# A list of weights for every step of a planned kernel, the last two token tiles finished singly, and epsilon added on VectorE

## Chip, cores and metric

The kernel runs on one core of a Trainium2 chip. The metric is the device time of one execution in microseconds (us); where several runs are compared, their median. Engines: TensorE (PE, its weight loads PEld), VectorE (DVE), ScalarE (ACT), GpSimd (POOL), SyncE (SP, which issues most transfers).

## What is computed

Two layers of gated cross-attention, each followed by a feed-forward network, on 2 x 1024 tokens of width 256, with a context of 77 tokens, 16 heads of 16. All inputs and outputs are float32. In short:

```python
x = x + tanh(g_xattn[0]) * attn0(layernorm(x), ctx)     # no biases, scale 16 ** -0.5
x = x + tanh(g_ffn[0])   * ffn0(layernorm(x))           # quantised: 256 -> 1024 -> gelu -> 256
x = x + tanh(g_xattn[1]) * attn1(layernorm(x), ctx, distances)   # biases, scores - log(d) * |s|
x = x + tanh(g_ffn[1])   * expert(layernorm(x))

def ffn0(x):     # both weights rounded to {-1, 0, 1} * mean|w|, activations to 8 bits per token
    h = gelu(quant_act(x) @ quant_weight(w1).T)
    return quant_act(h) @ quant_weight(w2).T

def expert(t):   # the router's weights are overwritten with 1 for expert 0
    y = t + relu(t @ w1[0] + b1[0]) @ w2[0] + b2[0]
    return (y - mean(y)) * rsqrt(var(y) + 1e-5) * gamma + beta
```

## The kernel before

**Tiling.** The 2048 tokens are 16 tiles of 128, taken in four groups of four (`GROUPS`, line 47). Each group passes four stages: attention of layer 0 (stage 0, `attention`, L718), the quantised network (stage 1, `bit_ffn`), attention of layer 1 (stage 2), the expert (stage 3, `expert_ffn`). A group's stages depend on each other; groups depend on one another only through shared buffers and engines.

**Attention.** The normalised tokens are transposed on TensorE (L602), multiplied with the query weights (L742), and for each half of the heads and each tile scored against the keys (L766), 8 heads x 77 keys in one row of 616. The softmax of such a row goes over the engines: bias (VectorE, L805, layer 1) or eviction (layer 0), maximum (VectorE, L814), subtraction (POOL or VectorE, L819), exponential (ScalarE, L828), sum (VectorE, L836), reciprocal (L841), product (POOL or VectorE, L845). The probabilities are transposed (L864), evicted (the helper `evict`, on ScalarE L373), multiplied with the values (L877) and the output weights (L898); VectorE adds the gated result to x (L906).

**Quantised network.** Products at L1069 (bf16) and L1099, gelu on ScalarE (L1077), maxima and rounding on VectorE (L995, L1004, L1050, L1085). **Expert.** Products in float32: the first at L1135 (eight blocks of 128 features, four tiles at once), the second at L1154, tile by tile. Two tiles share one PSUM bank `pp`; when both are done VectorE adds them to the normalised input (L1164), takes the statistics of both (`stats`, L535 and L536), and `inverse_std` (L541) gives one over the standard deviation; two VectorE operations per tile (L1174, L1181) and one store of both tiles on SyncE (L1188) end the pair.

**Inverse standard deviation.** It is one step of the plan on POOL with two operations, used by every normalisation: an addition of epsilon to the variance (L547) and a power of -0.5 (L548). There are 24 such steps: 16 for groups of four tiles and 8 for pairs of the expert.

**The order.** No loop of the code issues anything at once. Every operation is added to a `Plan` as a step with a planned cost, an engine (or two to choose from), what it reads and what it writes. `Plan.order(weight)` then simulates the engines: at each point it takes, on each engine, the steps that could start earliest, and among these the one with the highest weight; a step that needs a buffer waits until one is planned to be free. Weights only choose among steps that could start at the same planned moment. Transfers are taken in the order in which they were added. `Plan.issue` emits all steps in order of planned start, so each engine's instruction queue has the plan's order, and runs it in order, each instruction waiting for its semaphores. The plan's costs set the order only; they are no instructions.

Before, `Plan.best` (L297) makes the weight of a step from its longest chain of costs to the end, plus one number for its stage and group:

```python
weight = {
    s: rank[s] + OFFSET[s.stage[0]][s.stage[1]] - (SLACK if s.slack else 0.0)
    for s in self.steps
}
```

It then orders up to nine times, each time with weights from a backward pass (`Plan.back`) over the last order, and keeps the order with the earliest planned end.

Of the kernel before, what the change touches and what calls it, by code (L numbers as in the profile page):

```python
# [34 lines left out]
def bc(ap, axis, n):  # L35
# [14 lines left out]
T_EV, T_MX, T_SUB, T_DEN, T_MUL = 1, 1, 1, 1, 1  # L50

OFFSET = (
    (430, -41, -43, -161),
    (95, 126, -47, 121),
    (389, -35, -49, -189),
    (5, -32, 3, -328),
)
SLACK = 20.0
PASSES = 8
# [75 lines left out]
class Plan:  # L135
# [129 lines left out]
    def back(self, weight):  # L265


        todo = {s: len(s.before) for s in self.steps}
        ready = {e: [(s, 0.0) for s in self.steps if s.engine == e and not todo[s]] for e in LAG}
        free, ends, table = dict.fromkeys(ready, 0.0), {}, None  # L270
        while len(ends) < len(self.steps):
            best = None
            for e, waiting in ready.items():
                if waiting:
                    first = min(max(at, free[e]) for _, at in waiting)
                    pick = max(
                        (s for s, at in waiting if max(at, free[e]) <= first),
                        key=lambda s: weight[s],
                    )
                    if best is None or first < best[0]:  # L280
                        best = first, pick
            begin, s = best
            ends[s] = free[s.engine] = begin + s.cost
            if s.table and s.table != table:
                ends[s] = free[s.engine] = begin + s.cost + TABLE
                table = s.table
            ready[s.engine] = [w for w in ready[s.engine] if w[0] is not s]
            for a in sorted(s.after, key=lambda a: a.n):
                todo[a] -= 1
                if not todo[a]:  # L290
                    at = max(
                        ends[b] + (LAG[a.engine] if a.engine != b.engine else 0.0) for b in a.before
                    )
                    ready[a.engine].append((a, at))
        return ends

    def best(self):  # L297


        rank, best = {}, None  # L300
        for s in reversed(self.steps):
            rank[s] = s.cost + LAG[s.engine] + max((rank[b] for b in s.before), default=0.0)
        weight = {
            s: rank[s] + OFFSET[s.stage[0]][s.stage[1]] - (SLACK if s.slack else 0.0)
            for s in self.steps
        }
        for _ in range(PASSES + 1):
            done, given = self.order(weight)
            end = max(begin + s.cost for begin, s, _ in done)
            if best is None or end < best[0]:  # L310
                best = end, done, given
            weight = self.back({s: begin + s.cost for begin, s, _ in done})
        _, done, given = best
        for _, s, way in done:
            s.way = way
        return [(begin, s) for begin, s, _ in done], given
# [19 lines left out]
def tile_gated_cross_attention_stack(  # L336
# [204 lines left out]
    def inverse_std(mv, n, shifted=True):  # L541

        r = lazy(sm, [P, n], F32, "rstd", 4)
        shift = lazy(sm, [P, n], F32, "shift", 4)

        def fn():
            nc.gpsimd.tensor_scalar(r.ap, mv.ap[:, :, 1], EPS, None, ALU.add)  # L547
            nc.gpsimd.tensor_tensor(r.ap, r.ap, minus_half.ap[:, :n], ALU.pow)  # L548

        pool(1.4, fn, [mv, minus_half], [r])  # L550
        if shifted:
            dve(
                0.44,
# [562 lines left out]
    def expert_ffn(g):  # L1116
# [30 lines left out]
        for i, t2 in enumerate(both):  # L1147
# [19 lines left out]
            for j in range(2):  # L1167
                stats(tgt[2 * i + j], mv2, j)
# [147 lines left out]
```

## Time and profile before

| | before |
|---|---|
| median of 3 runs | 378.0 us (376.08 to 378.7) |
| the profiled execution's own time | 376.4 us |
| its span, first to last instruction | 374.7 us |
| mean granted TensorE clock | 0.976 |
| instructions | 5887 |
| PE busy | 338.2 us |
| DVE, ACT, POOL busy | 276.2, 244.2, 236.4 us |
| ScalarE table loads | 15, each 1283 ns |

The profile is of one execution. Its page gives busy times, the span in 40 slices (one digit each, in tenths, 9.4 us per slice), the costliest groups of instructions with their line, shape, count, total and mean, and the idle time before them with what ended it. Windows give the busy time of each engine in a stretch, waits say who waited for whom, and the timeline lists instructions in order of time. Matmul records come two to a float32 product; a busy TensorE isn't always one at its peak rate.

### The profile page before, as it was taken

What the parts mean: (1) busy time and instruction counts of PE and PEld (TensorE: products, weight loads), DVE (VectorE), ACT (ScalarE), POOL (GpSimd) and SP (SyncE); (2) the same over time, 40 slices, a digit from 0 to 9 for tenths busy, and PEclk for the clock granted to TensorE, in tenths of its full rate; (3) what the DMA queues carried; (4) which work ended last, traced back from release to release, by engine and by line L of the source; (5) the groups of instructions that cost most, each with busy time, mean ns of one, the idle gap of its engine ahead of it and who ended that gap; (6) DMA issues with size and microseconds to landing.
All of it is one profiled execution on the core that took longest, in us unless ns stands there. A gap on an engine that the chain in (4) does not pass through costs nothing.

```text
span 374.7 us, 5887 instructions
## 1 busy us (share of the span) xinstructions
PE 338.2 (90%) x2156; PEld 213.8 (57%) x2156; DVE 276.2 (74%) x580; ACT 244.2 (65%) x389; POOL 236.4 (63%) x252
## 2 busy tenths in 40 slices
PE   4967798699999699799999999899999998999991
PEld 4534365357555358455655666664488547584581
DVE  2699979999999979999797589995009888245033
ACT  3598799997969999998856374867313455324300
POOL 6599999847869834968997264778005858226011
PEclk9989989899999899999999999999999999999997
DMA  8993203000010000000000000001000000000001
GB/s 244 330 213 44 77 41 114 0 2 0 10 10 2 1 2 0 3 0 2 0 2 1 2 0 3 0 2 56 0 2 0 29 30 0 3 29 28 0 16 43
DMA packets 18131, 12.51 MB, mean 33 GB/s; under 512 B 8628, under 2 KB 17589, under 8 KB 18101
## 3 DMA queue, kind: packets, MB, share of 16 engines
q1 hardware_dynamic: 17012, 11.08, 10.7%
q10 hardware_dynamic: 1088, 1.05, 0.9%
q8 instruction: 17, 0.28, 0.3%
q14 instruction: 14, 0.11, 0.1%
HBM read 9.71 MB, written 2.10 MB: 32 GB/s over the span
## 4 chain that ended last, share of the span: by engine, by line
PE 54%; DVE 29%; ACT 7%; POOL 5%; issue 3%; DMA 1%; POOLq 0%; DVEq 0%; ACTq 0%
PE b L1154 15%; PE b L1135 13%; DVE den L836 5%; PE b L877 5%; DVE mx L814 5%; PE b L864 5%; PE b L898 4%; PE sc L766 3%; DVE st L535 3%; PE b L742 3%; DVE top_h L995 2%; POOL probs L845 2%; POOL probs L819 2%; DVE probs L805 2%; DVE hs L1085 2%
## 5 line engine op out<-in xcount | busy, mean ns | idle before, releaser
L819 POOL TENSOR_TENSOR probs<-probs,mx 128x616 f32<-128x616 f32 x64 | 78.6, 1240 | 31.2 <-DVE mx L814 23.9
L845 POOL TENSOR_TENSOR probs<-probs,den 128x616 f32<-128x616 f32 x64 | 77.5, 1230 | 6.5 <-DVE den L841 5.2
L864 PE MATMUL b<-ident,probs 128*128 128x128 f32 (+1 forms) x320 | 48.1, 288 | 12.9 <-ACT hs L1077 4.0
L1154 PE MATMUL b<-staged,hT 128*128 128x256 f32 x256 | 59.1, 381 | 0.4 <-ACT hT L373 0.4
L1135 PE MATMUL b<-xnT,staged 128*128 128x512 f32 x128 | 57.1, 596 | 0.3 <-ACT xnT L373 0.3
L547 POOL TENSOR_SCALAR rstd<-mv 128x4 f32<-128x4 f32 (+1 forms) x24 | 7.9, 328 | 71.9 <-DVE mv L536 65.8
L836 DVE TENSOR_REDUCE den<-probs 128x8 f32<-128x616 f32 x64 | 49.1, 771 | 5.5 <-ACT probs L828 5.5
L864 PEld LDWEIGHTS b<-ident,probs 128*128 128x128 f32 (+1 forms) x320 | 36.1, 143 | 29.8 <-issue 7.7
L1154 PEld LDWEIGHTS b<-staged,hT 128*128 128x128 f32 x256 | 47.5, 190 | 8.8 <-issue 2.1
L814 DVE TENSOR_REDUCE mx<-probs 128x8 f32<-128x616 f32 x64 | 49.3, 781 | 4.0 <-ACT probs L373 3.1
L373 ACT ACTIVATE pT<-b 128x512 f32<-128x512 f32 (+1 forms) x80 | 43.2, 603 | 3.2 <-PE b L864 2.9
L573 ACT ACTIVATE xn<-x,shift,rstd 128x256 f32<-128x256 f32 x48 | 25.5, 601 | 27.6 <-DVE shift L554 27.6
L1135 PEld LDWEIGHTS b<-xnT,staged 128*128 128x128 f32 x128 | 23.8, 190 | 28.0 <-issue 26.1
L373 ACT ACTIVATE hT<-b,eb_sb 128x512 f32<-128x512 f32 x32 | 21.8, 685 | 24.7 <-PE b L1135 24.6
L742 PE MATMUL b<-xnT,wq_sb 128*128 128x512 f32 x64 | 34.3, 643 | 2.9 <-ACT v L373 2.4
L877 PE MATMUL b<-pT,vbd 128*32 128x512 f32 (+1 forms) x256 | 31.5, 598 | 0.3 <-ACT hqT L1034 0.3
L898 PE MATMUL b<-wo_sb,OT 128*128 128x256 f32 x128 | 30.5, 382 | 0.4 <-DVE x L906 0.4
L805 DVE TENSOR_TENSOR probs<-sc,dbias 128x616 f32<-128x616 f32 x32 | 25.0, 784 | 7.4 <-PE sc L766 7.4
L535 DVE BATCH_NORM_STATS2 st<-x 128x6 f32<-128x256 f32 x64 | 24.9, 416 | 7.0 <-DMA x<-in_x_dram 6.0
L828 ACT ACTIVATE probs<-probs 128x616 f32<-128x616 f32 x32 | 22.8, 718 | 10.9 <-POOL probs L819 10.7
L906 DVE SCALAR_TENSOR_TENSOR x<-b,gates,x 128x512 f32<-128x512 f32 x16 | 11.7, 733 | 24.1 <-PE b L898 24.1
L766 PE MATMUL sc<-kbd,qT 32*128 32x154 f32 x512 | 28.5, 328 | 0.9 <-ACT probs L373 0.6
(100 smaller groups left out, 544.4 us busy)
## 6 DMA issues: line engine op xcount, KB each, us to landing
staged<-in_ew_dram SPq DMA_DIRECT2D x2, 1024.0 KB
out_dram<-x SPq DMA_DIRECT2D x8, 256.0 KB
x<-in_x_dram SPq DMA_DIRECT2D x6, 256.0 KB
staged<-in_fw1T_dram SPq DMA_DIRECT2D x1, 1024.0 KB
staged<-in_fw2T_dram SPq DMA_DIRECT2D x1, 1024.0 KB
dbias<-in_dist_dram SPq DMA_DIRECT2D x1, 616.0 KB
x<-in_x_dram SPq DMA_DIRECT2D x4, 128.0 KB
wk_sb<-in_wkT_dram ACTq DMA_DIRECT2D x1, 256.0 KB
```

The lines of the kernel that those rows point to most:

```text
L373: nc.scalar.activation(out(), src(), AF.Relu if relu else AF.Copy if bias is None else AF.Identity, bias=0.0 if bias is None else bias(), ...
L742: lambda h=h, k=k, pq=pq: nc.tensor.matmul(pq.ap, wq_sb.ap[:, k, h * P : (h + 1) * P], xnT.ap[:, k, :], start=(k == 0), stop=(k == KT - 1),),
L766: nc.tensor.matmul(sc.ap[:, q, j * QK : j * QK + QK], qT.ap[rows, h, at : at + P], kbd.ap[rows, h, b].rearrange("p h s -> p (h s)"), start ...
L814: lambda j, n: nc.vector.tensor_reduce(each(mx, j, n), heads(j, n), AX.X, ALU.max),
L819: lambda e, j, n: e.tensor_tensor(heads(j, n), heads(j, n), bc(each(mx, j, n), 2, SK), ALU.subtract),
L836: lambda j, n: nc.vector.tensor_reduce(each(den, j, n), heads(j, n), AX.X, ALU.add),
L845: lambda e, j, n: e.tensor_tensor(heads(j, n), heads(j, n), bc(each(den, j, n), 2, SK), ALU.mult),
L864: lambda j=j, c=c, m=m, tr=tr: nc.tensor.transpose(tr.ap[:m, j, :], prs[j // 2].ap[:, j % 2, c * P : c * P + m], ident.ap),
L877: nc.tensor.matmul(po.ap[32 * q : 32 * q + 32, :], vbd.ap[: CH[c], b, h, s, :], pTs[c].ap[: CH[c], :], start=(i < 4), stop=(i >= 4),)
L898: nc.tensor.matmul(pp.ap[:, j % 2, :], OT.ap[:, k, j * P : (j + 1) * P], wo_sb.ap[:, k, :], start=(k == 0), stop=(k == KT - 1),)
L1135: lambda f=f, k=k, ph=ph: nc.tensor.matmul(ph.ap, ew1_sb.ap[:, k, f * P : (f + 1) * P], xnT.ap[:, k, :], start=(k == 0), stop=(k == KT - 1),),
L1154: lambda j=j, f=f, pp=pp: nc.tensor.matmul(pp.ap[:, j % 2, :], hT[f].ap[:, j * P : (j + 1) * P], ew2_sb.ap[:, f, :], start=(f == 0), stop= ...
```

## The change

**A weight for each step.** `OFFSET`, `SLACK`, `PASSES`, the chain lengths and `Plan.back` are gone. A list of 2088 numbers between 0 and 1869 gives each step its weight by its number in the order in which steps are added, and the plan is ordered once. The list laid over the steps gives these means:

| stage | group 0 | group 1 | group 2 | group 3 |
|---|---|---|---|---|
| 0, attention of layer 0 | 1613 | 1172 | 946 | 1033 |
| 1, quantised network | 1363 | 1052 | 500 | 1041 |
| 2, attention of layer 1 | 1227 | 1057 | 173 | 485 |
| 3, expert | 789 | 681 | 723 | 220 |

**Planned costs** of some steps are new: transposes 0.13 instead of 0.15 and 0.14, the value products 1.90 instead of 1.97, the first quantised product 0.54 instead of 0.44, and a few on VectorE. Five constants that were all 1 (`T_EV` and others) are written as 1.

**Epsilon.** In `inverse_std` the addition becomes a step of its own on VectorE, ahead of the power on POOL.

**The last two tiles.** Of the last pair of the last group, each tile is added, measured, scaled and stored by itself: the addition, `inverse_std` and the store are issued once per tile, on half the size. All other pairs stay as they were. The steps now name single tiles of the shared buffers as what they touch.

```diff
-OFFSET = (
-    (430, -41, -43, -161),
...
+WEIGHTS = tuple(
+    int(w) for w in """
+1628 1470 1670 1643 995 733 467 1247 1143 1461 1551 1018 1411 1503 1814 1347 1543 1583 1841 1823
...
     def best(self):
...
+        weight = {s: WEIGHTS[s.n] for s in self.steps}
+        done, given = self.order(weight)
...
-    def inverse_std(mv, n, shifted=True):
+    def inverse_std(mv, n, shifted=True, part=None):
...
-        def fn():
-            nc.gpsimd.tensor_scalar(r.ap, mv.ap[:, :, 1], EPS, None, ALU.add)
-            nc.gpsimd.tensor_tensor(r.ap, r.ap, minus_half.ap[:, :n], ALU.pow)
-
-        pool(1.4, fn, [mv, minus_half], [r])
+        at = part or slice(0, n)
+
+        dve(
+            0.12, lambda: nc.vector.tensor_scalar(r.ap, mv.ap[:, at, 1], EPS, None, ALU.add),
+            [(mv, j) for j in range(at.start, at.stop)], [r],
+        )
+        pool(
+            1.0,
+            lambda: nc.gpsimd.tensor_tensor(r.ap, r.ap, minus_half.ap[:, :n], ALU.pow),
+            [minus_half, r], [r],
+        )
...
+            last = g == len(GROUPS) - 1 and i == n // 2 - 1
+            for part in ((slice(0, 1), slice(1, 2)) if last else (slice(0, 2),)):
+                count = part.stop - part.start
+                js = range(2 * i + part.start, 2 * i + part.stop)
+                keys_of = lambda t: [(t, j % 2) for j in js]
                 dve(
+                    0.12 + 0.29 * count,
+                    lambda t2=both[i], pp=pp, part=part: nc.vector.tensor_tensor(
+                        t2.ap[:, part], pp.ap[:, part], t2.ap[:, part], ALU.add
                     ),
+                    keys_of(pp) + keys_of(both[i]), keys_of(both[i]),
+                )
+                for j in js:
+                    stats(tgt[j], mv2, j % 2)
+                r2, _ = inverse_std(mv2, count, False, part)
...
+                dma(
+                    0.5,
+                    lambda x2=x_pairs[g][i], part=part, at=(FIRST[g] + js[0]) * P,
+                    count=count: nc.sync.dma_start(
+                        out=out[ds(at, count * P), :].rearrange("(j p) d -> p j d", p=P),
+                        in_=x2.ap[:, part],
                     ),
+                    keys_of(x_pairs[g][i]), [],
+                )
```

## The prediction

> **What bounds the kernel now.** I read the page's busy shares and slices first, then the table of windows, then TensorE's (PE's) waits, and last the timeline of the end.
>
> The page:
>
> ```profile
> PE 338.2 (90%) x2156; PEld 213.8 (57%) x2156; DVE 276.2 (74%) x580; ACT 244.2 (65%) x389; POOL 236.4 (63%) x252
> ...
> PE   4967798699999699799999999899999998999991
> ...
> DVE  2699979999999979999797589995009888245033
> ...
> PEclk9989989899999899999999999999999999999997
> ```
>
> TensorE is nearest to full, but two halves hide in the mean: up to slice 19 (about 180 us) DVE (VectorE) stands at 7 to 9 and PE has holes; after it PE is full and DVE has whole slices of 0 to 3. The windows put numbers on it (length, then busy time of PE, PEld, DVE, ACT, POOL, then clock):
>
> ```profile
> core 0: us, PE busy (x) PEld busy (x) DVE busy (x) ACT busy (x) POOL busy (x), PEclk, DMA share, GB/s
> 0.00:10.00 10.00, 5.25 (x23) 4.52 (x24) 2.67 (x9) 3.06 (x6) 6.50 (x25) 1.00 0.81 242
> 10.00:60.00 50.00, 41.26 (x296) 24.18 (x298) 44.28 (x93) 42.12 (x64) 44.30 (x41) 0.93 0.55 150
> 60.00:90.00 30.00, 26.25 (x227) 15.08 (x223) 28.12 (x54) 28.71 (x46) 20.73 (x25) 0.94 0.01 2
> 90.00:180.00 90.00, 82.29 (x624) 50.00 (x626) 84.32 (x183) 82.09 (x130) 67.77 (x69) 0.98 0.02 3
> 180.00:360.00 180.00, 176.37 (x971) 114.44 (x968) 110.20 (x228) 88.24 (x146) 94.75 (x92) 1.00 0.03 10
> ```
>
> PE idles 4.75 us before the first weights arrive, then 8.7, 3.8, 7.7 and 3.6 us in the four windows that follow, and 7.9 us after its last product (374.7 - 366.8). So 23.8 us lie between its first and last matmul, 20.2 of them before 180 us, where VectorE is 89 to 94% busy and ScalarE 84 to 96%. Up to 180 us the softmax and quantising engines set the pace; after it TensorE does. The longest waits of PE are short and scattered:
>
> ```profile
> PE b L623 <- DMA wk_sb<-in_wkT_dram: 4.8, 1, 4.8
> PE b L864 <- ACT hs L1077: 4.0, 4, 2.3
> PE b L864 <- ACT pT L373: 3.6, 3, 1.4
> PE b L742 <- ACT v L373: 2.4, 1, 2.4
> ```
>
> No single wait can be removed to win much; only other work put into the holes can. That work exists:
>
> ```profile
> L1154 PE MATMUL b<-staged,hT 128*128 128x256 f32 x256 | 59.1, 381 | 0.4 <-ACT hT L373 0.4
> L1135 PE MATMUL b<-xnT,staged 128*128 128x512 f32 x128 | 57.1, 596 | 0.3 <-ACT xnT L373 0.3
> ```
>
> These are the expert products, 116 us, a third of all PE time, with very little work for others. The first one starts at 175.2 us, and the window from 339 to 367 us is group 3's alone: PE 27.8 of 28 us, DVE 7.6.
>
> **Part 1, the weights.** Nothing is removed from any engine; only the order moves. Along the list, group 0 keeps its lead (means 1613, 1363, 1227), its expert products get 1292 (first half) and 641 (second), and what now stands last is layer-1 attention of groups 3 and 2 (485 and 173) and group 2's quantised FFN (500), beside the experts of groups 0, 1, 2 (789, 681, 723). So VectorE-heavy attention of two groups is put late, where VectorE has room (110 of 180 us busy), and PE-only products are offered as fillers as soon as they are ready. That is the direction that the two halves ask for. What it can win at most: the 23.8 us of holes, and the clock that they cost. The granted clock of 0.93, 0.94 and 0.98 on 41.3, 26.3 and 82.3 us busy is 2.9 + 1.6 + 1.6 = 6.1 us. Ceiling: 29.9 us.
>
> How much of it is filled I estimate window by window. 10 to 60 us: only layer 0 is runnable, and DVE, ACT and POOL are all at 84 to 89% there: a quarter of 8.7, 2.2 us. 60 to 90 us: half of 3.8, 1.9 us. 90 to 180 us: attention of several groups can be mixed with the first expert products: two thirds of 7.7, 5.1 us. After 180 us: half of 3.6, 1.8 us. Together 11.0 us. The clock by the same shares: 0.7 + 0.8 + 1.1 = 2.6 us. **Part 1: -13.6 us**, between -29.9 (all filled) and a loss, priced under the rivals. One cost is not in the trace: mixing gelu of one group with exp of another reloads ScalarE's table. Before there are 15 loads at 1283 ns (19 us). Ten more would be 13 us of ScalarE, nothing where it is 49% busy (after 180 us), a hole on PE where it is 91% busy (90 to 180). This I leave in the range.
>
> **Part 2, the last two tiles.** The end of before:
>
> ```profile
> 366.19 0.59 PE L1154 MATMUL b<-staged,hT 128*128 128x256 f32 x2
> 366.89 0.69 DVE L1164 TENSOR_TENSOR xn<-b,xn 128x512 f32<-128x512 f32 x1 [2.94 <-PE b L1154]
> 367.62 0.75 DVE L535 BATCH_NORM_STATS2 st<-xn 128x6 f32<-128x256 f32 x2
> ...
> 368.68 0.37 POOL L547 TENSOR_SCALAR rstd<-mv 128x2 f32<-128x2 f32 x1 [5.64 <-DVE mv L536]
> 369.13 0.81 POOL L548 TENSOR_TENSOR rstd<-rstd,minus_half 128x2 f32<-128x2 f32 x1
> 369.98 0.88 DVE L1181 SCALAR_TENSOR_TENSOR x<-xn,rstd,x 128x256 f32<-128x256 f32 x2 [0.61 <-POOL rstd L548]
> 370.94 0.37 SPq L1188 DMA_DIRECT2D out_dram<-x  x1
> ```
>
> From the last matmul (366.78) to the store's issue (370.94) are 4.16 us. For one tile: hop 0.11; the addition on half the columns 0.42 (0.69 less half of what 128x512 costs over 128x256, by 0.73 at L906 against 0.47 at L1107); one statistic 0.38 and its aggregate 0.15; epsilon on VectorE 0.15; hop 0.09; the power 0.75; hop 0.04; one final product 0.44. Sum 2.53, so -1.6 us. The first of the two tiles has its own chain of 2.5 us under the second tile's 16 matmul records at 0.216 (5.18 us for 24), 3.5 us, and is done in time; it adds an addition, a power and a store, all hidden. SyncE gains one issue of 0.37 us, ahead of the last store but 3 us early. The store itself: from issue to the span's end are 3.76 us for 256 KB, now 128 KB. In proportion to bytes that would be -1.9 us. The Trainium skill (DMA: Bandwidth & Descriptors, Anatomy of one DMA) speaks against this: a fixed 2.0 us, mostly the receipt of the write, and only bytes over 436 GB/s on top, so halving gives -0.3 us (its fit is for transfers issued from GpSimd; these go out on SyncE). No row separates the two; I take -0.3. **Part 2: -1.9 us** (-3.5 by proportion; about 0 if another group's store ends last).
>
> **Part 3, epsilon on VectorE.** Off POOL go 24 operations (7.9 us, mean 328 ns), onto VectorE come 25. Nearest row: the tensor_scalar at L1004, 150 ns on 128x1, 410 ns on 128x4 with two operations; the reciprocal on 128x4 takes 178. I take 0.18: 4.5 us of VectorE in all (3.8 to 10). The chain for the norm loses 0.29 + 0.08 on POOL and gains 0.18, but on VectorE the step queues behind whatever is there, often a reduction of 0.78 us (L814) with ScalarE's normalisation (L573) and so the transposes waiting behind. Some 12 of the 25 lie before 180 us, 2.2 us of an engine at 93%; half of it I count: **+1 us** (-1.5 to +4). A rule would make it worse: the Trainium skill (SBUF — State Buffer, Who interferes with whom) says that tensor_scalar on VectorE can take the port pair shared with GpSimd, and that the later one then blocks for the whole instruction. With POOL busy two thirds of the time in pieces of 1.22 us, each of 25 additions would wait 0.4 us on average, +10 us on VectorE, some +4 on the end. The rows speak otherwise: L1004 is the same operation beside the same POOL, and its 16 instances of 128x1 lie within 123 and 156 ns. I keep the row.
>
> The new planner costs and the folded constants issue no other instruction; their effect is in the order, part 1.
>
> **Sum.** -13.6 - 1.9 + 1.0 = -14.5 us on 376.4 us (span 374.7 and 1.7 around it) gives 361.9. The runs' median of 378.0 lies 1.6 above the profiled execution; made against it, **363 us**.
>
> **The rivals.**
> A, the forecast, 355 to 370 us: chance 0.63. For it: two halves with opposite limits, and 116 us of fillers. Against: the list only ranks steps that could start at the same time, and the chip's queues run in order whatever comes late.
> B, nearly all holes and clock filled: 378.0 - 29.9 - 1.9 + 1 = 347, centre 350: 0.12. Against it: the start, where nothing but layer 0 is runnable.
> C, the holes only move (more table loads, epsilon behind reductions, VectorE still full before 180 us): parts 2 and 3 are left, 377 us: 0.12.
> D, slower: the end becomes VectorE's and POOL's. Eight half-pairs of softmax on layer 1 cost POOL 8 x (1.24 + 1.23) = 20 us and VectorE 8 x 2.5 (0.78 at L805, 0.78 at L814, 0.77 at L836, 0.20 at L841) = 20 us per group; if the expert products of groups 0, 1 and 3 have been used up when group 2's layer-1 attention (weight 173) runs, PE has only that group's own transposes and waits for about half, 10 us, with the same again for group 3, and gains nothing earlier: 378 - 1.9 + 1 + 13 to 20, about 392. It decides once PE's idle time after 250 us (about 2 now) exceeds the 13.6 us gained earlier. For it: weights 173 and 485 stand after the experts. Against: those experts have 116 us to lie beside 40. Chance 0.13.
>
> **Range and chances.** Leaving out the lower half of B (0.07) and D (0.13): 351 to 378. A measurement of this kernel tells about 1% from no change. Faster by over 1%: A, B and a little of C, 0.76; within 1%: 0.12; slower: 0.12.
>
> **What would show it.** Part 1 right: PE idle before 180 us down from 25 (start included) towards 15, PE clock there at 0.97 or more, expert products (L1135's) before 150 us, VectorE busier after 180 us. Part 2: last matmul to store's issue near 2.5 us, issue to end about 3.5. Part 3: VectorE's new additions at 0.15 to 0.2 us. Wrong if the table loads pass 25, if PE waits on attention after 250 us (D), or if before 180 us VectorE is still full and PE as empty as now (C).

## The result and the profile after

The changed kernel takes 382.2 us (median of 4 runs, 381.0 to 384.6) against 378.0: ratio 1.013, interval 1.010 to 1.016. It is 1.3% slower; 363 us and a range that ended at 378 had been forecast. The profiled execution of after is the slowest of its four, 384.6 us with a span of 382.5; that of before, 376.4 us with a span of 374.7, is near the fastest of its own. So the two profiles lie 7.8 us apart, the medians 4.2. The page of after, shares of the span first:

```profile
PE 341.9 (89%) x2147; PEld 215.1 (56%) x2156; DVE 291.8 (76%) x608; ACT 244.5 (64%) x389; POOL 228.5 (60%) x227
...
PE   4975998799798898899999998989999899999992
...
DVE  2698999979999999999856999988238984174033
...
PEclk9996899899899999999999999999999989999998
```

The line to look at is not PE's. ACT stays at 244 us and POOL gives up 7.9 us with the epsilon additions, as reckoned. DVE rises from 276.2 to 291.8 us, by 15.6, and only some 4.5 had been reckoned for the new steps. PE's digits before slice 19 are no fuller than they were. The windows of after, cut as before's were, with one more at the end (length, busy time of PE, PEld, DVE, ACT, POOL, then clock):

```profile
10.00:60.00 50.00, 41.10 (x292) 25.86 (x290) 44.05 (x85) 40.34 (x62) 42.19 (x35) 0.90 0.48 139
60.00:90.00 30.00, 26.88 (x205) 14.35 (x208) 26.71 (x57) 26.88 (x44) 18.92 (x22) 0.94 0.12 26
90.00:180.00 90.00, 79.65 (x611) 49.89 (x614) 86.51 (x185) 81.98 (x129) 63.28 (x61) 0.98 0.01 1
180.00:360.00 180.00, 173.97 (x961) 108.06 (x962) 124.92 (x255) 91.08 (x152) 95.74 (x85) 0.99 0.03 10
```

Between 90 and 180 us PE is busy for 79.7 us where it was busy for 82.3, and DVE for 86.5 of 90 where it was 84.3. Up to 180 us PE idles 27.2 us (25.0 before; 15 was forecast), after it 13.4 (11.5). That is 4.1 us more idle time, of which at most 2 us may be nine products whose records are missing in the trace of after (2147 against 2156, each 0.21 us behind the next). The mean granted clock is 0.976 in the profile of before and 0.969 in that of after, but this belongs to the two executions shown and not to the change: over all executions before was granted 0.961 to 0.976 and after 0.968 to 0.972. The first expert product starts at 176.6 us, where it started at 175.2: no filler reached the holes before 150 us. The table loads are still 15.

TensorE's waits of after, in us in total, times and the longest:

```profile
PE b L914 <- ACT xnT L418: 6.4, 1, 6.4
PE b L673 <- DMA wk_sb<-in_wkT_dram: 4.8, 1, 4.8
PE b L914 <- POOL probs L895: 2.5, 4, 0.9
...
PE sc L816 <- DVE den L891: 2.3, 1, 2.3
```

Two are new. The 6.4 us stand at 26 us, where ScalarE has a logarithm (1.32 us) and two table loads (1.28 us each) ahead of the evictions that PE needs. The 2.3 us stand at 304 us, and lead to VectorE.

**Where VectorE's 15.6 us are.** The same work by line and shape, first in before, then in after (count, busy us, mean ns):

```profile
L1181 DVE SCALAR_TENSOR_TENSOR x<-xn,rstd,x 128x256 f32<-128x256 f32 x16 | 12.1, 795 | 4.6 <-POOL rstd L548 4.6
L1174 DVE SCALAR_TENSOR_TENSOR xn<-xn,mv,gamma_sb 128x256 f32<-128x256 f32 x16 | 8.5, 570 | 0.0
L1050 DVE TENSOR_SCALAR xn<-xn,up_x 128x256 f32<-128x256 f32 x16 | 6.5, 463 | 0.1
L1004 DVE TENSOR_SCALAR top_h<-top_h 128x1 f32<-128x1 f32 x16 | 2.4, 150 | 0.4
L1004 DVE TENSOR_SCALAR top_x<-top_x 128x4 f32<-128x4 f32 x4 | 1.6, 410 | 0.1
```

```profile
L1240 DVE SCALAR_TENSOR_TENSOR x<-xn,rstd,x 128x256 f32<-128x256 f32 x16 | 10.9, 712 | 1.9 <-POOL rstd L598 1.9
L1232 DVE SCALAR_TENSOR_TENSOR xn<-xn,mv,gamma_sb 128x256 f32<-128x256 f32 x16 | 10.1, 648 | 0.3
L1100 DVE TENSOR_SCALAR xn<-xn,up_x 128x256 f32<-128x256 f32 x16 | 9.7, 663 | 0.1
L593 DVE TENSOR_SCALAR rstd<-mv 128x4 f32<-128x4 f32 x16 | 3.7, 230 | 0.4
L895 DVE TENSOR_TENSOR probs<-probs,den 128x616 f32<-128x616 f32 x2 | 3.5, 1806 | 0.0
L593 DVE TENSOR_SCALAR rstd<-mv 128x2 f32<-128x2 f32 x7 | 3.1, 440 | 0.1
L1054 DVE TENSOR_SCALAR top_x<-top_x 128x4 f32<-128x4 f32 x4 | 2.7, 675 | 0.1
```

Of the 15.6 us, some 7 are the new epsilon additions (L593), 3.5 two products of the softmax that the new plan gives to VectorE (L895; none in before), 3.2 the quantising step (L1050, now L1100). One operation on one shape has no fixed duration here: L1100 takes 299 to 1372 ns. Its instances sort by what GpSimd does as they start. Two instances of L604 (128x4) in the timeline of after, each with the GpSimd operation in progress (start, length):

```profile
236.51 1.22 POOL L895 TENSOR_TENSOR probs<-probs,den 128x616 f32<-128x616 f32 x1
236.57 1.17 DVE L604 SCALAR_TENSOR_TENSOR shift<-mv,rstd 128x4 f32<-128x4 f32 x1
```

```profile
136.03 0.31 POOL L1059 TENSOR_SCALAR down_h<-top_h,s_w 128x1 f32<-128x1 f32 x1
...
136.58 0.15 DVE L604 SCALAR_TENSOR_TENSOR shift<-mv,rstd 128x4 f32<-128x4 f32 x1
```

The operation on four elements per partition lasts as long as the rest of GpSimd's softmax, and ends with it. Some instances of after, from the trace's single records (the seven that began during a GpSimd operation all do this):

```
L604, ns            rest of GpSimd's operation    L604 lasted
at 236.57 (L895)    1156                          1173
at 293.05 (L869)     958                           973
at 158.48 (L895)     825                           843
at 184.92 (L1175)    710                           730
at  97.04 (L895)     581                           599
no such operation      0                           109 to 165
```

So VectorE operations of some kinds wait for GpSimd when both read SBUF. That is what the Trainium skill states (SBUF — State Buffer, Who interferes with whom): an instruction of VectorE with two inputs in SBUF contends with one of GpSimd that reads SBUF, and one in a two-port mode is blocked for the whole instruction; a reduction is not. The trace agrees for GpSimd's large operations (its small ones are in the last section): the two-input L604 and L1240, and the tensor_scalar L1100 and L593, last longer by up to 1.1 us; the reductions L864 and L886 stay between 0.74 and 0.80 us beside the same operations. Counted over L604 and the kinds of operation in the rows of after above, 18 of 64 instances in before and 34 of 91 in after last over a quarter longer than when free, beside an operation of GpSimd on 128x616 or 128x512.

The place at 302 us shows how this reaches TensorE. VectorE and GpSimd in after:

```profile
301.46 1.22 POOL L895 TENSOR_TENSOR probs<-probs,den 128x616 f32<-128x616 f32 x1 [0.92 <-DVE den L891]
...
301.90 2.47 DVE L1240 SCALAR_TENSOR_TENSOR x<-xn,rstd,x 128x256 f32<-128x256 f32 x2
302.64 1.45 POOL L1175 TENSOR_TENSOR xn<-xn,eb_sb 128x512 f32<-128x512 f32 x1
304.29 0.78 DVE L864 TENSOR_REDUCE mx<-probs 128x8 f32<-128x616 f32 x1
```

Two final products take 2.47 us where they take 0.88 at the end, behind GpSimd twice; the softmax of the next half-pair is queued behind them and starts 1.6 us late, and TensorE waits 2.3 us until VectorE has read the last scores and their buffer is free for the next.

**The end.** The last VectorE work and store of after, and the split pair:

```profile
344.31 3.29 PE L1204 MATMUL b<-staged,hT 128*128 128x256 f32 x14 [0.59 <-DVE xn L1220]
...
375.25 0.69 DVE L1220 TENSOR_TENSOR xn<-b,xn 128x512 f32<-128x512 f32 x1 [2.95 <-PE b L1204]
...
378.13 0.88 DVE L1240 SCALAR_TENSOR_TENSOR x<-xn,rstd,x 128x256 f32<-128x256 f32 x2 [0.20 <-POOL rstd L598]
379.09 0.38 SPq L1248 DMA_DIRECT2D out_dram<-x  x1
```

The pair that ends last is whole (128x512, two final products): it is group 2's. The split pair is group 3's and is done by 350 us. There, TensorE itself waited 0.59 us for the first tile's addition before it went on with the second tile.

### The profile page after: what moved, and what is told of

It reads as the page before. It is cut to its first block, busy times and chain, and to the rows that moved or that the text cites. A ratio compares the mean times of both kernels' runs of the same rounds, so it can differ in the third digit from the quotient of the medians.

```text
span 382.5 us, 5851 instructions
## 1 busy us (share of the span) xinstructions
PE 341.9 (89%) x2147; PEld 215.1 (56%) x2156; DVE 291.8 (76%) x608; ACT 244.5 (64%) x389; POOL 228.5 (60%) x227
## 4 chain that ended last, share of the span: by engine, by line
PE 44%; DVE 38%; ACT 10%; issue 3%; POOL 2%; DMA 1%; POOLq 0%; DVEq 0%; ACTq 0%
PE b L1185 10%; PE b L1204 9%; PE b L914 5%; DVE mx L864 5%; DVE den L886 5%; PE b L927 5%; DVE st L580 4%; PE b L792 3%; DVE probs L855 3%; DVE top_h L1045 3%; ACT probs L878 3%; DVE xn L1100 2%; PE sc L816 2%; PE b L948 2%; DVE x L956 2%
## 5 line engine op out<-in xcount | busy, mean ns | idle before, releaser
L869 POOL TENSOR_TENSOR probs<-probs,mx 128x616 f32<-128x616 f32 x64 | 77.4, 1222 | 27.1 <-DVE mx L864 23.5
L895 POOL TENSOR_TENSOR probs<-probs,den 128x616 f32<-128x616 f32 x62 | 76.8, 1254 | 23.9 <-DVE den L891 10.0
L598 POOL TENSOR_TENSOR rstd<-rstd,minus_half 128x4 f32<-128x4 f32 (+2 forms) x25 | 25.1, 1004 | 70.2 <-DVE rstd L593 68.6
L914 PE MATMUL b<-ident,probs 128*128 128x128 f32 (+1 forms) x320 | 52.2, 290 | 13.0 <-ACT xnT L418 6.4
L1185 PE MATMUL b<-xnT,staged 128*128 128x512 f32 x128 | 59.9, 612 | 0.1
L914 PEld LDWEIGHTS b<-ident,probs 128*128 128x128 f32 (+1 forms) x320 | 37.6, 144 | 33.4 <-POOL probs L895 11.3
L886 DVE TENSOR_REDUCE den<-probs 128x8 f32<-128x616 f32 x64 | 49.0, 777 | 4.7 <-ACT probs L878 4.4
L864 DVE TENSOR_REDUCE mx<-probs 128x8 f32<-128x616 f32 x64 | 48.6, 780 | 3.1 <-ACT probs L418 2.7
L418 ACT ACTIVATE pT<-b 128x512 f32<-128x512 f32 (+1 forms) x80 | 44.4, 601 | 9.0 <-PE b L914 8.7
L927 PE MATMUL b<-pT,vbd 128*32 128x512 f32 (+1 forms) x256 | 32.4, 623 | 0.1
L580 DVE BATCH_NORM_STATS2 st<-x 128x6 f32<-128x256 f32 x64 | 25.8, 414 | 7.1 <-DMA x<-in_x_dram 6.1
L816 PE MATMUL sc<-kbd,qT 32*128 32x154 f32 x512 | 27.5, 324 | 2.3 <-DVE den L891 2.3
L816 PEld LDWEIGHTS sc<-kbd,qT 32*128 32x128 f32 x512 | 19.1, 188 | 14.8 <-issue 7.2
```

The source lines that it names most:

```text
L418: nc.scalar.activation(out(), src(), AF.Relu if relu else AF.Copy if bias is None else AF.Identity, bias=0.0 if bias is None else bias(), ...
L580: dve(0.39, lambda: nc.vector.bn_stats(st.ap, src.ap), [src], [st])
L816: nc.tensor.matmul(sc.ap[:, q, j * QK : j * QK + QK], qT.ap[rows, h, at : at + P], kbd.ap[rows, h, b].rearrange("p h s -> p (h s)"), start ...
L864: lambda j, n: nc.vector.tensor_reduce(each(mx, j, n), heads(j, n), AX.X, ALU.max),
L869: lambda e, j, n: e.tensor_tensor(heads(j, n), heads(j, n), bc(each(mx, j, n), 2, SK), ALU.subtract),
L886: lambda j, n: nc.vector.tensor_reduce(each(den, j, n), heads(j, n), AX.X, ALU.add),
```

## The experiments

The theories: the loss is the new order's (O); it is epsilon's on VectorE (E); it is the split's; and then, inside O, P: VectorE's waits for the port that it shares with GpSimd took what the order had gained. N, in the later runs, is the view that the port has nothing to do with it. Ratios are to before.

**1 and 2: epsilon.** On after, epsilon goes back to GpSimd with the order kept; on before, it alone goes to VectorE.

```diff
-            0.12, lambda: nc.vector.tensor_scalar(r.ap, mv.ap[:, at, 1], EPS, None, ALU.add),
+            0.12, lambda: None,
...
+            nc.gpsimd.tensor_scalar(r.ap, mv.ap[:, at, 1], EPS, None, ALU.add)
```

> The changed kernel with its order kept exactly, but epsilon added on POOL again, in front of the power. Theory O (the new order is what costs: VectorE runs later than planned and TensorE waits for it): time stays within 1.5 us of the changed kernel, 380 to 383. Theory E (epsilon on VectorE costs, 7 us of VectorE busy with waits for the port pair included): most of the 4 to 5 us loss is gone, 376 to 378.

Measured: 384.2 us, ratio 1.017 (1.015 to 1.019). Undoing it does not help: 2 us more, if anything (the intervals of e1 and after just overlap).

```diff
-            nc.gpsimd.tensor_scalar(r.ap, mv.ap[:, :, 1], EPS, None, ALU.add)
+            nc.vector.tensor_scalar(r.ap, mv.ap[:, :, 1], EPS, None, ALU.add)
```

> The kernel before with its order kept exactly, but epsilon added on VectorE, at the place where POOL did it. Theory O: within 1.5 us of before, 377 to 379.5. Theory E: 381 to 384.

Measured: 378.9 us, ratio 1.0028 (1.0015 to 1.0041), +1.1 us. E, which expected 381 to 384, is out as the cause.

**3 and 4: the split.** On before, group 3's last pair is finished tile by tile; on after, group 2's last pair too, the one that ends last.

```diff
+                    for h, (st, ag, gm, fin) in enumerate(own):
+                        one = slice(h, h + 1)
+                        nc.vector.tensor_tensor(
+                            t2.ap[:, one], pp.ap[:, one], t2.ap[:, one], ALU.add
+                        )
...
+                        nc.sync.dma_start(
+                            out=out[ds(at + h * P, P), :].rearrange("(j p) d -> p j d", p=P),
+                            in_=x2.ap[:, one],
+                        )
```

> The kernel before with its order kept, but the last pair of group 3 (the one that ends last there) added, measured, scaled and stored tile by tile. The prediction's chain of 2.5 instead of 4.16 us and a smaller last store: 1.9 us less, 376. If the size of the store decides nothing: 1.6 less. If the first tile's addition can't run beside the second tile's products: about 0.5 less or nothing.

Measured: 378.7 us, ratio 1.0031 (1.0021 to 1.0041): slower, where even the worst case had no loss.

> The changed kernel with its order kept; group 2's last pair, which ends last there, is finished tile by tile as well. If the split of the changed kernel only hit the wrong pair: 1.6 to 1.9 us less than the changed kernel, 380.5. If it gains nothing anywhere: as the changed kernel, 382.

Measured: 383.3 us, ratio 1.015 (1.013 to 1.017): nothing gained. The end of e3 says why:

```profile
365.75 2.75 PE L1154 MATMUL b<-staged,hT 128*128 128x256 f32 x12
368.61 0.42 DVE L1202 TENSOR_TENSOR xn<-b,xn 128x256 f32<-128x256 f32 x1 [2.94 <-PE b L1154]
...
371.41 0.41 DVE L1202 TENSOR_TENSOR xn<-b,xn 128x256 f32<-128x256 f32 x1
```

The first tile's addition starts when the products of both tiles are done; two chains of 2.9 us then run one behind the other.

**5: epsilon without waits.** A reduction of one element takes the place of the addition, so that it can't wait for the port; epsilon is left out.

```diff
-            0.12, lambda: nc.vector.tensor_scalar(r.ap, mv.ap[:, at, 1], EPS, None, ALU.add),
+            lambda: nc.vector.tensor_reduce(r.ap, mv.ap[:, at, 1:2], AX.X, ALU.add),
```

> The changed kernel, order kept; the epsilon step on VectorE is a copy of the variance by a reduction over one element instead of a tensor_scalar (it leaves epsilon out). In the runs so far reductions on VectorE never lasted longer than their usual time, tensor_scalar did (up to 1.2 us instead of 0.17). Theory P (VectorE instructions that wait for POOL's port eat the plan's gain): the 25 steps take 0.1 to 0.2 us each without outliers, 1 to 2 us less than the changed kernel, 380 to 381. Theory O (the order is bad by itself): no difference, 382.

Measured: 382.3 us, ratio 1.013 (1.010 to 1.015), as after and not the 1 to 2 us less that P expected. The step did become free of waits, on the shapes that took 230 and 440 ns in after:

```profile
L594 DVE TENSOR_REDUCE rstd<-mv 128x4 f32<-128x4 f32 x16 | 2.5, 156 | 0.5
L594 DVE TENSOR_REDUCE rstd<-mv 128x2 f32<-128x2 f32 x7 | 1.1, 150 | 0.1
```

So the waits of this one step are not on the path.

**6 and 7: GpSimd without reads.** In both kernels GpSimd's two softmax operations become two fills of the same row, which take as long (1.26 us on average for two, against 1.22) but read nothing; the softmax of those rows is left out.

```diff
+            def filled(e, j, n):
+                for _ in range(2):
+                    e.memset(flat(j, n), 0.01)
...
-                lambda e, j, n: e.tensor_tensor(
+                lambda e, j, n: filled(e, j, n) if e is nc.gpsimd else e.tensor_tensor(
```

> The kernel before, order kept; POOL's two softmax operations (subtraction of the maximum, product with the reciprocal of the sum) are each replaced by two fills of the same row, so that POOL is about as long at work but reads no SBUF (the softmax is left out on POOL). Theory P: VectorE's operations with two SBUF operands no longer wait; little changes in this order, which has less of it on its path: 1 to 3 us less, 375 to 377. Theory O: the same gain here as in the changed kernel.

Measured: 377.1 us, ratio 0.9993 (0.9976 to 1.0010). The page of e6:

```profile
PE 338.9 (90%) x2156; PEld 216.4 (57%) x2156; DVE 270.7 (72%) x580; ACT 244.8 (65%) x389; POOL 235.7 (63%) x380
```

VectorE is busy for 5.5 us less than in before, yet the time hardly falls: the waits of before's order were not on its path.

> The same replacement in the changed kernel (the softmax is left out on POOL), order kept. Theory P: the waits at the addition of the normalised tiles, the quantising step and the shift shrink, and 5 to 11 us come back: 371 to 377, not above the kernel before with the same replacement. Theory O: as much less as in the kernel before, so still 4 to 5 us above it.

Measured: 375.4 us, ratio 0.994 (0.992 to 0.997). The page of e7 and its row for the shift:

```profile
PE 338.5 (91%) x2156; PEld 213.9 (57%) x2156; DVE 278.0 (75%) x608; ACT 243.8 (65%) x389; POOL 226.0 (61%) x353
```

```profile
L604 DVE SCALAR_TENSOR_TENSOR shift<-mv,rstd 128x4 f32<-128x4 f32 x12 | 3.5, 293 | 2.3 <-POOL rstd L598 2.3
```

GpSimd is as busy as in after (226.0 against 228.5 us) and only the softmax's reads are gone. VectorE is busy for 278.0 us, 7.3 more than in e6, where with the reads it was 15.6 more than in before: about half of the rise, 8.3 us, goes with the reads. Before gains 0.3 us by the edit, after 7.0 (ratios 1.0128 and 0.9942, on 378). With the reads the new order loses 4.8 us; without them it wins 1.9 over before's. TensorE's idle time in the span says the same: 36.5 us in before and 38.0 in e6, 40.6 in after (38.7 if the missing records are added) and 34.0 in e7. P holds, and these are the two runs that show it: the sign of the change turns on what GpSimd does in the softmax. Reading SBUF is the one thing meant to differ. Not parted from it: the second fill no longer waits for VectorE's reciprocal (0.19 us), and TensorE multiplies other numbers; both are the same in e6 and e7.

**8: measured mean durations.** A new list, searched for with the mean durations of VectorE's and ScalarE's steps in after's trace as planned costs.

> The changed kernel with another list of weights and with planned costs for VectorE and ScalarE that are the mean times from the changed kernel's trace, waits for the port included (epsilon 0.22 instead of 0.12, quantising step 0.58 instead of 0.38, the last two operations of a norm 0.58 and 0.68 instead of 0.43); list found by trying lists against these costs. All other code is the changed kernel's. Theory P: a list made with the true VectorE times keeps its gain: 368 to 374, below both kernels. Theory O (a list of single weights is worth nothing on the chip, whatever its costs): 378 or more.

Measured: 378.1 us, ratio 1.0016 (0.9999 to 1.0033). Four us better than after, but not the 368 to 374 that P expected: VectorE is again busy for 290.7 us, with other instructions waiting now. A mean doesn't say when the port is taken, and the waits move with the order.

**9 and 10: a plan that knows the port.** The planner gets the rule itself: a VectorE step of a kind that waits (`SHARES`) is planned to end later when it would begin during a GpSimd step of a kind that holds it up (`TAKES`). The control is searched for without it.

```diff
+            if (s.n, s.way) in SHARES and port[0] <= begin < port[1]:
+                cost += max(0.0, port[1] - begin - 0.18)
+            if (s.n, s.way) in TAKES:
+                port = begin, begin + cost
```

> After's code, but with a new list of weights, made by a search that knows the port: in Plan.order a VectorE step of a kind that the traces show waiting (two operands in SBUF, or a wide tensor_scalar) that would begin during one of GpSimd's two softmax operations or its bias additions is planned to end later by the rest of that operation less 0.18 us; the durations are measured ones, those of the waiting kinds taken where nothing held them up. Nothing else differs, and the output is the reference's. Replayed with these rules, after's order ends at 376.3 us with 20.9 us of such waits (its trace has 21.7 us), the list of e8 at 371.8, and this one at 365.0 with 14.8. The first two had spans some 4.5 us longer than replayed, so theory P (the new order lost its gain to VectorE's waits for the port) expects here a span of about 369.5 and 371 us (369 to 374), ratio 0.976 to 0.99, and VectorE busy for some 284 us instead of 291.8. Theory N (the list's gain is lost to differences between plan and chip of many kinds, and any list that is searched for lands at about 378) expects what e8 gave, 377 to 381.

Measured: 373.1 us, ratio 0.988 (0.986 to 0.991), VectorE busy for 286.0 us.

> The control of the list that knows the port: the same code, the same search of the same length from the same starting order and with the same spread of trial durations, but the planner doesn't know the port; each kind of VectorE and ScalarE step has its mean duration in the trace of after, waits for the port included. Without the port its replay ends at 367.9, with it at 371.4 with 19.2 us of waits. Theory P expects a span of about 376 and 377.6 us (375.5 to 380), VectorE busy for 288 to 291, and a distance to the list that knows the port of 4 to 8 us. Theory N expects the two within 2 us of each other.

Measured: 380.1 us, ratio 1.006 (1.004 to 1.009). One correction: the list of e9 had in fact been searched for three times as long, so this pair was not a fair one; and in the profiles most of the 7 us lies in the clock, granted at 0.83 in e10 between 10 and 60 us, at 0.93 in e9. Hence the next three. One thing differs that the expectations of e9 and e13 leave out: a constant of the planner, `EASE`, which keeps steps with two possible engines off VectorE, was 4 in after and is 36.5 in e9, 35.6 in e13, 18.9 in e10, 2.2 in e14 and 2.1 in e15. In the softmax it moves little: GpSimd does 127 or 128 of the 128 subtractions and products of the softmax in all five.

**13 to 15: fair pairs.** Same start, seed and length of search within a pair.

> The fair partner of e10_list_mean: a list from a search that knows the port, from the same starting order, with the same seed and the same length of search (the list of e9 was searched for three times as long). Nothing else differs, and the output is the reference's. Replayed with the port it ends at 367.0 us with 10.3 us of waits for the port; e9 and e10 had spans 7.3 and 7.2 us longer than replayed (365.0 and 371.4). Theory P expects a span of 374.2 and 375.9 us (374 to 378), ratio 0.99 to 1.0, and 2 to 6 us less than e10. Theory N (what a list gains or loses on the chip has nothing to do with the port) expects no fixed sign: anything from 373 to 381.

Measured: 375.2 us, ratio 0.993 (0.990 to 0.995); 4.9 us less than its partner e10.

> A second list from a search that knows the port, from before's order as the starting order and with another seed, of the same length as that of e10. Replayed with the port it ends at 369.5 us with 15.1 us of waits. Theory P expects a span of 376.7 and 378.4 us (376 to 381), and 2 to 6 us less than its control e15_mean_other. Theory N expects no fixed sign between the two.

Measured: 376.5 us, ratio 0.997 (0.994 to 0.999).

> The control of e14_port_other: same starting order, seed and length, but a search that doesn't know the port and takes each kind's mean duration in after. Replayed with the port it ends at 373.6 us with 18.3 us of waits. Theory P expects a span of 380.8 and 382.5 us (379 to 385). Theory N expects no fixed sign against e14.

Measured: 382.1 us, ratio 1.013 (1.009 to 1.016); e14 is 5.5 us faster. The pages of e10 and e13, then of e15 and e14:

```profile
PE 342.0 (90%) x2156; PEld 215.8 (57%) x2156; DVE 288.3 (76%) x606; ACT 247.6 (65%) x391; POOL 231.9 (61%) x229
...
PEclk9996599999999699999999999999999999999998
```

```profile
PE 334.6 (90%) x2147; PEld 211.8 (57%) x2156; DVE 282.2 (76%) x606; ACT 245.5 (66%) x389; POOL 229.9 (62%) x229
...
PEclk9998999999998999999999999999999999999997
```

```profile
PE 342.7 (90%) x2147; PEld 216.0 (57%) x2156; DVE 289.6 (76%) x607; ACT 245.8 (65%) x388; POOL 228.4 (60%) x229
...
PEclk9996959899989989999999999999999999999998
```

```profile
PE 338.4 (90%) x2147; PEld 214.5 (57%) x2156; DVE 291.7 (78%) x614; ACT 247.2 (66%) x387; POOL 228.5 (61%) x227
...
PEclk9996899989999899999999999999999999999999
```

Both pairs have the expected sign and size, and the three lists that know the port are the only ones here that beat before. But the pairs don't show that it is the port. TensorE's idle time in the span is the same within each pair, to about 1 us: 36.6 us in e10 and 37.7 in e13 (35.8 with its nine missing records), 37.8 in e15 and 37.6 in e14. What differs is how long its products take (342.0 against 334.6 us, 342.7 against 338.4), and with it the mean granted clock (0.964 against 0.983, 0.959 against 0.977). Between 10 and 60 us it was 0.83 in both controls, 0.97 in e13 and 0.90 in e14. VectorE of e14 is even busier than that of its control. That VectorE's waits made the clock lower is not shown, so what these lists say for P stays an argument; e6 and e7 carry it.

How VectorE's excess goes with the time (duration of each operation over the lower quartile of its shape in before and after, summed):

```
                 before  after  e8    e10   e15   e9    e13   e14
excess, us       20.9    30.2   30.4  28.9  28.5  25.2  21.4  26.6
time, us         378.0   382.2  378.1 380.1 382.1 373.1 375.2 376.5
```

Excess alone doesn't order the times (e8 has as much as after).

**11 and 12: a bank for the second tile.** e3 again, but the last tile's products go to another buffer of PSUM, the memory that TensorE writes to, in another of its banks; then the same for group 2's last pair on the list of e9.

```diff
+            own_bank = pp
+            if g == len(GROUPS) - 1 and i == n // 2 - 1:
+                own_bank = bank("pp", (P, 2, D))
...
-                        lambda j=j, f=f, pp=pp: nc.tensor.matmul(
-                            pp.ap[:, j % 2, :], hT[f].ap[:, j * P : (j + 1) * P],
+                        lambda j=j, f=f, b=own_bank if j % 2 else pp: nc.tensor.matmul(
+                            b.ap[:, j % 2, :], hT[f].ap[:, j * P : (j + 1) * P],
```

> Before, order kept, group 3's last pair finished tile by tile as in e3_before_split, but the last tile's products go to a bank of PSUM of their own (one of the other three buffers of the same pool, the one whose last use is earliest). If the shared bank is what made the first tile's addition wait for all the products of both tiles in e3, that addition now starts when the first tile's products end, its chain lies beside the last tile's products, and after the last matmul only one tile's chain of about 2.8 us is left instead of 4.16 for the pair in before: -1.4 us, and -0.2 for a store of half the size: 376.1 us, ratio 0.994 to 0.998. If something else serialises them (the order of the semaphores, the small tiles that both use, VectorE still full), the first addition starts again after the last product and the result is e3's, ratio 1.003.

Measured: 375.9 us, ratio 0.9956 (0.9940 to 0.9972). Its end:

```profile
364.68 3.40 PE L1166 MATMUL b<-staged,hT 128*128 128x256 f32 x15
...
365.17 0.42 DVE L1214 TENSOR_TENSOR xn<-b,xn 128x256 f32<-128x256 f32 x1
...
368.19 0.42 DVE L1214 TENSOR_TENSOR xn<-b,xn 128x256 f32<-128x256 f32 x1
...
370.59 0.48 DVE L1193 SCALAR_TENSOR_TENSOR x<-xn,rstd,x 128x256 f32<-128x256 f32 x1 [0.77 <-POOL rstd L1220]
```

The first addition (365.17) now lies under the second tile's products, which end at 368.08 (364.68 + 3.40). From there to the store's issue 3.0 us remain, 4.16 in before, and from the issue to the end 2.9 instead of 3.76.

> The list that knows the port (e9_list_port), with the last pair of group 2, the one that ends last in it, finished tile by tile and with a bank of PSUM of its own for the last tile's products, as in e11_before_split_banks; epsilon of these two tiles is added on VectorE. In e9 the time from the pair's last matmul to its last VectorE operation is 4.1 us, in e11 it is 3.0 with epsilon on GpSimd. If the two causes are independent, this takes another 1.0 to 1.7 us off 373.1: 371.4 to 372.1 us, ratio 0.982 to 0.987 to before. If the split only pays where VectorE was idle in before's order, it stays at 373.

Measured: 372.0 us, ratio 0.984 (0.982 to 0.986): the fastest version here, 6 us under before and 10 under after. It is 1.1 us under e9 by the medians, 1.6 by the ratios, near the 1.0 to 1.7 expected.

## Why the prediction was wrong

**Part 1 (-13.6 us) is the step that failed.** It gave shares of the holes to fillers and took VectorE's work as fixed ("nothing is removed from any engine; only the order moves"). The plan's own end does fall, from 370.8 to 362.0 us. But an order also decides which VectorE steps begin while GpSimd reads, and the prediction put nothing for that. In after more of them do (34 instances, 18 in before): VectorE's excess grows by 9.3 us, of which 2.9 are on the new epsilon additions and 2.0 on the two products moved to VectorE. By place, 2.3 of the 9.3 us lie before 180 us, where VectorE was up to 94% full and 9.2 us of holes were to be filled, and 7.0 after it, in the part where the prediction had counted on room. TensorE's idle time did not fall by the 11.0 us forecast but rose, by 4.1 us as recorded: 2.2 before 180 us and 1.9 after it. e6 and e7 put 6.7 us (7.0 less 0.3) on GpSimd's reads in the softmax, enough to turn the sign. Rival C named one of the two places, "VectorE still full before 180 us", but not this reason, and set its end at 377. Rival D foresaw a slower kernel, with VectorE and POOL behind it, but by another path: from 250 us to the last product TensorE idles 4.6 us (1.2 in before), where D wanted over 13.6.

**The rule that was weighed and dropped decided.** Part 3 set the Trainium skill's rule on the shared port against L1004, "the same operation beside the same POOL", and kept the row. The row was read in one of its two forms. On 128x1 it never waits (138 to 154 ns where GpSimd's softmax runs). On 128x4 its mean of 410 ns was put down to its two operations; the trace of before has two instances of 631 and 671 ns that began with 608 and 645 ns of L845 left, and two of 169 ns that began beside nothing. The longest of them:

```profile
65.55 1.22 POOL L845 TENSOR_TENSOR probs<-probs,den 128x616 f32<-128x616 f32 x1
...
66.12 0.67 DVE L1004 TENSOR_SCALAR top_x<-top_x 128x4 f32<-128x4 f32 x1
```

So the counterexample stood in the other form of the same line. A page fits the difference: in VectorE: DVE Perf Modes, What auto-detection actually checks, the two-port mode asks for outermost dimensions above one that are even or equal, and 128x1 has none above one. That 128x1 is outside the mode for this reason is our reading; no run shows the mode itself. Applying the rule to the epsilon steps alone (+10 us of VectorE) would also have missed: their additions wait some 3 us in all (7.1 us against 25 at 0.16), and e5 finds that off the path. It had to be applied to every VectorE step with two inputs in SBUF and every tensor_scalar on more than one element, and to what the new order puts beside it.

**Part 2 (-1.9 us) failed twice.** Its own reservation, "about 0 if another group's store ends last", came true. And where the split pair does end last (e3) it costs 1.2 us, since the claim that the first tile's chain lies under the second tile's products does not hold: both tiles lie in one buffer that fills one bank (2 x 256 float32, 2 KiB). The Trainium skill (PSUM — Partial Sum Buffer, PSUM bank collisions raise a hardware error) says that access must be guarded by bank, not by address; the traces show it as the addition at 368.61 in e3 and as TensorE's 0.59 us at 344 in after. e11 gives the second tile another buffer and another bank at once, so it does not tell which of the two makes the wait. With it the total was right, -1.7 us against the forecast -1.9, in part by luck: the chain gave 1.1 us instead of 1.6, since epsilon stayed on GpSimd there, and the smaller store 0.5 to 0.9 instead of the 0.3 taken from the page (2.8 to 2.9 us from issue to the end in e3, e11 and e12, 3.4 to 3.8 for whole pairs in before, after and e9, one execution each).

**Part 3 (+1.0 us) was right in size** for before's order: +1.1 in e2, with additions at 158 and 162 ns where 180 were taken. In after's order the additions take 230 and 440 ns on average, for the port, and still it is no loss: with epsilon on GpSimd the kernel is some 2 us slower (e1).

**What stays open.** Without the reads the new order wins 1.9 us, not the 8.8 of the two plans. Some waits remain in e7 (its bias additions still read, its fills still hold up the tensor_scalar L1104: 573 ns on average against 341 when free); TensorE's wait of 6.5 us at 25 us also remains. How much each costs was not tried. The lists of e8 to e15 end 8 to 12 us later on the chip than in their own plans, before's only 4. And the lower clock of the lists that don't know the port was seen, not explained.

## What to carry to other kernels

A planned duration is only a property of an instruction if no other engine can hold it up; before an order is changed, list an operation's durations one by one, and look at what the neighbour engine was doing in the long ones. When a rule is weighed against a row, test the rule on the form of the row that meets its conditions, not on the nearest line number. Here splitting the last pair paid once its second tile had a buffer and bank of its own and the pair was the one that ends last.

## What the runs showed of the hardware

- A VectorE operation with two SBUF inputs that begins during a GpSimd operation on 128x616 or 128x512 ends some 15 to 20 ns after it on 128x4, where it takes about 160 ns when free, and 280 ns after it on 128x256, where it takes about 480 (L1240 in after: rest 1207, lasted 1490). So such a wait costs the rest of GpSimd's operation less some 0.15 to 0.2 us. An operation that is done before that point is not held up.
- GpSimd's power and its small tensor_scalar didn't do this, though they read SBUF: in before L1181 took 455 and 476 ns with 1015 and 641 ns left of the power on 128x4 (L548), and in after L1100 took 349 ns with 389 ns of L1059 (128x4) left. Here the measurement differs from the page, which says it of any GpSimd instruction that reads SBUF.
- GpSimd's fills (628 ns on average) leave two-input operations free: in e7 the five instances of L604 that began during one took 111 to 161 ns, and its two long ones, 811 and 1191 ns, began during bias additions (average 293 ns, 569 in after). The tensor_scalar on 128x256 is held up by fills too: 445 to 783 ns for the instances that began with 300 ns or more of a fill left.
